# A quantised feed-forward behind two attentions: last norm by token tiles, first inputs prepared in the attention, maxima by quarters, and work shared among DVE, ACT and POOL

## The chip, the cores and the metric

One core of one Trainium2 chip. The metric is the device time of one execution in microseconds (us): 3412.78 before, the median of three runs (3411.16 to 3414.15). PE is the matmul engine; DVE, ACT and POOL work on vectors; SP issues the DMAs. SBUF is the on-chip memory, PSUM holds what PE writes.

## What is computed

Eight batches of 512 tokens, 256 wide, go through four steps; LN is a layer norm without weights:

```
x = x + attention0(LN(x), ctx)      # 16 heads of 64, 1024 context tokens
x = x + experts(LN(x))              # two of eight expert MLPs, chosen by the first token
x = x + attention1(LN(x), ctx)      # 16 heads of 16
x = x + quantised_ffn(LN(x))        # 256 -> 1024 -> 256

def quantised_ffn(x):
    hidden = gelu(a16(x) @ w8(W_in) + b_in)
    return a16(hidden) @ w8(W_out) + b_out
def a16(x):                         # one scale for the whole tensor, all batches
    scale = 32767 / max(|x|)
    return round(x * scale) / scale
```

The maximum in a16 runs over all eight batches. So the feed-forward can't begin with its first matmul before the last batch has left the second attention, nor with its second matmul before hidden is known for every batch.

## The kernel before

**Attention and experts.** Two streams of steps, written as generators, are woven into one order of PE work by a list of run lengths written out by hand (ORDER, weave): the first stream has the first attention of all batches, the second has weights, and for each batch experts, second attention and last norm (rest, L1234). The last batch's second attention is split between the two. PE follows this order; a scheduler orders what is on DVE, ACT, POOL and SP by the steps' place in the program and by what they need.

**project** (L1120) ends the second attention for a tile of 128 tokens (g is 0 to 3): two matmuls (L1123, cacc), and DVE adds the result to x (L1127).

**last_norm** (L1213) runs once a batch's four tiles are done. DVE takes mean and variance (L384, L385). POOL takes the inverse root by three Newton steps on 128x4 values (L387 to L398, about 14 instructions). DVE takes the largest and the smallest x of each token (ends, L1221), POOL subtracts the mean and multiplies by the root (L1223, L1226), which gives the token's largest normed values without norming it. SP stores x to memory (xd, L1231). Later, x is loaded again from there.

**Feed-forward, phase 1.** SP loads the quantised weights wi_q (512 KB, L1287) and wo_q (1 MB, L1289). one_scale (L1269) turns a column of maxima into one scale: a reduction, a transpose on PE, a reduction, a matmul that spreads the value, and the five small DVE instructions of scales (L299 to L302). inputs(b) (L1320) loads xd, norms it (L1325), scales and rounds it (L1333, by adding and keeping a large constant ROUND), splits the integer into two bf16 parts (L1335 and L1338), transposes both on PE (L1346, txq) and copies them to SBUF on ACT (L1347, xTf). For each b there are 32 matmuls 512 wide (L1359, fh), ACT's gelu in eight pieces (L1368) into hid[b], which stays in SBUF, and one DVE reduction of 128x4096 for the maximum (L1378).

**Phase 2**, for each b: load xd again; POOL adds the bias b_out in four instructions (L1388); DVE scales and adds ROUND in two halves (L1392, h); ACT takes ROUND away in four pieces of 128x1024 (L1395, unround); ACT makes hi, rounded to PE's fp32r format (L1401), eight of 128x512; DVE makes the rest, lo (L1402), eight of 128x512; PE does 64 matmuls 256 wide (L1407, fo); DVE joins the product with x (L1416), SP stores the output. The first matmuls need h, unround, hi and lo in this order. The pieces hi and lo lie in a pool of seven buffers (tag "p", L1315). x has three buffers (L125).

Of the kernel before, what the change touches and what calls it, by code (L numbers as in the profile page):

```python
# [8 lines left out]
F32 = mybir.dt.float32  # L9
# [69 lines left out]
def kernel(  # L79
# [75 lines left out]
    xs, xd = {}, {}  # L155
    stats = const.tile([P, B, NT, 2], F32, name="stats")

    ends = const.tile([P, B, 2, NT], F32, name="ends")

    def load_x(b, src=None):  # L160
        t = xpool.tile([P, NT, D], F32, tag="x", name=f"x{b}")
# [68 lines left out]
    cbv_b = wts.tile([P, D], F32, name="cbv_b")  # L230
    cbo_b = wts.tile([P, D], F32, name="cbo_b")
    bo_b = wts.tile([P, D], F32, name="bo_b")

    COPIED = [(0.3, "s", "act", 0.4, "full")]

    def second_weights():

        room = kvp.tile([P, 4, DH, D], F32, tag="cv", name="room", bufs=1)
        nq, nv, no = (room[:, i] for i in range(3))
        nv = nv[:, :, :DC]  # L240
        nc.sync.dma_start(out=nq, in_=c_wq.rearrange("(c p) n -> p c n", p=P))
        nc.sync.dma_start(out=nv, in_=c_wv.rearrange("(c p) n -> p c n", p=P))
        nc.sync.dma_start(out=no, in_=c_wo.rearrange("(c p) n -> p c n", p=P))
        rows = kvp.tile([1, 4, D], F32, tag="ck", name="bias_rows")
        for i, src in enumerate((c_bq, c_bv, c_bo, a_bo)):
            nc.sync.dma_start(out=rows[:, i, :], in_=src.unsqueeze(0))
        yield 30, [(0.5, "s", "dve", 0.3, "one")]
# [12 lines left out]
        for i, dst in ((3, bo_b), (1, cbv_b), (2, cbo_b)):  # L260
            yield 0, [(0.5, "s", "dve", 0.4, "one")]
            t = bank(f"tbo{i}")
            nc.tensor.matmul(t[:, :D], ones_r, rows[:, i, :], start=True, stop=True)
            nc.vector.tensor_copy(dst, t[:, :D])
        done.add("biases")
# [114 lines left out]
    def norm_stats(b, mv, rs):  # L380

        st = small.tile([P, NT, 6], F32, tag="st", name="st")
        for t in range(NT):
            nc.vector.bn_stats(st[:, t, :], xs[b][:, t, :])  # L384
            nc.vector.bn_aggr(mv[:, t, :], st[:, t, :])  # L385
        ve = small.tile([P, NT], F32, tag="ve", name="ve")
        nc.gpsimd.tensor_scalar(ve, mv[:, :, 1], EPS, None, ALU.add)  # L387

        r = small.tile([P, NT], F32, tag="r0", name="r0")
        nc.gpsimd.tensor_scalar(  # L390
            r.bitcast(I32), ve.bitcast(I32), -0.5, float(0x5F3759DF), ALU.mult, ALU.add
        )
        t1 = small.tile([P, NT], F32, tag="t1", name="t1")
        for i in range(3):
            nc.gpsimd.tensor_tensor(t1, r, r, ALU.mult)
            nc.gpsimd.tensor_tensor(t1, t1, ve, ALU.mult)
            nc.gpsimd.tensor_scalar(t1, t1, -0.5, 1.5, ALU.mult, ALU.add)
            nc.gpsimd.tensor_tensor(rs if i == 2 else r, r, t1, ALU.mult)  # L398

    def norm_of(b):  # L400
        mv = small.tile([P, NT, 2], F32, tag="mv", name="mv")
# [535 lines left out]
    def second_attention(b, pairs, last=False):  # L937
# [182 lines left out]
        def project(g, aT):  # L1120
# [4 lines left out]
                )  # L1125
            dst = xs[b][:, g, :]
            nc.vector.tensor_tensor(dst, acc[:, :D], dst, ALU.add)  # L1127

        def scores(p, kt):
            es[p, kt] = exponentials(  # L1130
# [82 lines left out]
    def last_norm(b):  # L1213


        yield 1, [(0, None, "dve", 5.5, None), (0, None, "pool", 4.5, "then")]
        mv = small.tile([P, NT, 2], F32, tag="mv", name="mv")
        norm_stats(b, mv, stats[:, b, :, 1])
        nc.vector.tensor_copy(stats[:, b, :, 0], mv[:, :, 0])
        for i, op_ in enumerate((ALU.max, ALU.min)):  # L1220
            nc.vector.tensor_reduce(ends[:, b, i, :], xs[b], AX.X, op_)  # L1221
        for i in range(2):
            nc.gpsimd.tensor_tensor(  # L1223
                ends[:, b, i, :], ends[:, b, i, :], stats[:, b, :, 0], ALU.subtract
            )
            nc.gpsimd.tensor_tensor(  # L1226
                ends[:, b, i, :], ends[:, b, i, :], stats[:, b, :, 1], ALU.mult
            )
# [63 lines left out]
    bor = fw.tile([1, D], F32, name="bor")  # L1292
    nc.sync.dma_start(out=bor, in_=f_bo.unsqueeze(0))

    amax_x = fw.tile([P, 1], F32, name="amax_x")
    nc.vector.tensor_reduce(
# [9 lines left out]
    t = bank("bbo")  # L1306
    nc.tensor.matmul(t[:, :D], ones_r, bor, start=True, stop=True)
    bo_b = fw.tile([P, D], F32, name="bo_b")
    nc.vector.tensor_copy(bo_b, t[:, :D])

    hp = ffn.enter_context(tc.tile_pool(name="hid", bufs=1))
    amax_h = fw.tile([P, B], F32, name="amax_h")

    def parts_of(shape, dtype, name):
        return hp.tile(shape, dtype, tag="p", name=name, bufs=7)  # L1315
# [1 line left out]

    COARSE = 512 * ROUND

    def inputs(b):  # L1320

        load_x(b, xd[b])
        xn = parts_of([P, NT, D], F32, f"xn_{b}")
        for t in range(NT):
# [5 lines left out]
                ALU.subtract,  # L1330
                ALU.mult,
            )
        nc.vector.tensor_scalar(xn, xn, s_x, ROUND, ALU.mult, ALU.add)  # L1333
        xq = parts_of([P, 2, NT, D], BF16, f"xq_{b}")
        nc.vector.tensor_scalar(  # L1335
            xq[:, 0], xn, COARSE - ROUND, COARSE, ALU.add, ALU.subtract
        )
        nc.vector.scalar_tensor_tensor(  # L1338
            xq[:, 1], xn, ROUND, xq[:, 0], ALU.subtract, ALU.subtract
        )  # L1340
# [11 lines left out]
    for b in range(B):  # L1352
        hid = hp.tile([P, NF, S], F32, tag=f"h{b}", name=f"h{b}")
        for f2 in range(NF // 2):
# [11 lines left out]
            for j in range(2):  # L1366
# [5 lines left out]
                    bias=bi[:, f : f + 1],  # L1372
                    scale=sc_i[:, f : f + 1],
                )
            if f2 == 1 and b + 1 < B:
                following = inputs(b + 1)
        xT = following
        nc.vector.tensor_reduce(  # L1378
            amax_h[:, b : b + 1], hid, AX.XY, ALU.max, apply_absolute_value=True
        )  # L1380
        hids.append(hid)

    s_h, inv_h = one_scale(amax_h, 32767.0, "h")
    for b in range(B):
        hid = hids[b]
        load_x(b, xd[b])
        for i in range(NT):
            nc.gpsimd.tensor_tensor(xs[b][:, i, :], xs[b][:, i, :], bo_b, ALU.add)  # L1388
        acc = ps_s.tile([P, 2, 512], F32, tag="s", name=f"fo_{b}")
        for half in range(2):  # L1390
            h = hid[:, half * 4 : half * 4 + 4, :]
            nc.vector.tensor_scalar(h, h, s_h, ROUND, ALU.mult, ALU.add)  # L1392
        for f2 in range(NF // 2):
            h = hid[:, 2 * f2 : 2 * f2 + 2, :]
            nc.scalar.activation(h, h, AF.Identity, bias=unround)  # L1395
            hi = parts_of([P, 2, S], F32R, f"hi_{b}_{f2}")
            lo = parts_of([P, 2, S], F32R, f"lo_{b}_{f2}")
            for j in range(2):
# [6 lines left out]
                for t in range(NT):  # L1405
                    for u in range(2):
# [8 lines left out]
        dst = xs[b].rearrange("p t d -> p (t d)")  # L1415
        nc.vector.scalar_tensor_tensor(  # L1416
            dst, acc.rearrange("p i n -> p (i n)"), inv_h, dst, ALU.mult, ALU.add
        )
        nc.sync.dma_start(out=out[b].rearrange("(t p) d -> p t d", p=P), in_=xs[b])
    ffn.close()  # L1420


# [49 lines left out]
```

## Time and profile before

| | us |
|---|---|
| median of 3 runs | 3412.78 |
| the profiled execution | 3413.37 |
| its span | 3411.5 |
| last sum on x in the attention, start | 3233.99 |
| first fh of phase 1 | 3250.4 |
| last gelu ends | 3317.9 |
| first h of phase 2 | 3324.9 |
| last lo ends | 3403.1 |

Times within the profile count from the span's start, so the phases behind the attention take 177.5 us of it. Groups of instructions are shown as: line, engine, operation, output <- inputs by the program's names, shapes, count, then busy time, the mean duration of one in ns, and after the second bar how long the engine had been idle just before them and what ended that idle time. Timelines give the start, the length of a row of instructions and their number. L12 is line 12 of the kernel. The profiled execution's granted TensorE clock was 0.974 of full speed.

### The profile page before, as it was taken

To read this page: it belongs to the slowest core of one execution; us is meant where nothing else is said; L and a number is where in the kernel's file an instruction comes from. 1 tells how busy PE (TensorE), PEld (TensorE's weight loads), DVE (VectorE), ACT (ScalarE), POOL (GpSimd) and SP (SyncE) were. 2 spreads that over 40 slices of the span, in tenths; PEclk is the share of its full clock that TensorE was granted. 3 is DMA by queue.
4 is the path that set the end of the run, shared out by engine and by line. 5 is a ranking of instruction groups with operands and counts; after the bars stand their busy time and mean duration, and the time that the engine had idled before them with its cause. 6 is when DMAs were issued, how large, how long until landed. Compare 5 with 4: busy or idle time off the path is not lost.

```text
span 3411.5 us, 59285 instructions
## 1 busy us (share of the span) xinstructions
PE 3183.9 (93%) x24293; PEld 1789.0 (52%) x24293; DVE 2045.0 (60%) x2583; ACT 1857.9 (54%) x2589; POOL 1282.3 (38%) x1260
## 2 busy tenths in 40 slices
PE   7899999999999999999999999999999999978887
PEld 4455555555455555555545554555555555544347
DVE  3654566546665476655665466654766456656688
ACT  4554456544556455554655455554555546544578
POOL 4355522454234622355224542345223543311002
PEclk9999999999999999999999999999999999988989
DMA  2010111011110111111110111101111111012112
GB/s 86 26 32 21 45 33 37 27 41 41 38 35 27 43 32 36 35 44 29 32 51 14 41 41 38 41 26 38 32 41 32 41 32 29 14 44 62 50 57 81
DMA packets 102649, 132.00 MB, mean 39 GB/s; under 512 B 19807, under 2 KB 82028, under 8 KB 102252
## 3 DMA queue, kind: packets, MB, share of 16 engines
q1 hardware_dynamic: 102380, 128.22, 13.7%
q8 instruction: 192, 3.15, 0.4%
q14 instruction: 77, 0.63, 0.1%
HBM read 67.34 MB, written 9.96 MB: 23 GB/s over the span
## 4 chain that ended last, share of the span: by engine, by line
PE 74%; DVE 12%; ACT 6%; POOL 3%; issue 2%; DMA 1%; SPq 1%; ACTq 0%; DVEq 0%; POOLq 0%
PE s L728 15%; PE av L699 11%; PE cav L1079 6%; PE t L676 6%; DVE cmx L531 5%; PE acc L486 5%; PE pv L512 4%; PE s_c L562 3%; PE pq L602 3%; PE pk L512 3%; ACT e L741 2%; ACT e_c L567 2%; PE sm_c L524 2%; PE s_c L565 2%; PE pv L514 2%
## 5 line engine op out<-in xcount | busy, mean ns | idle before, releaser
L758 POOL TENSOR_TENSOR e<-e,share 128x1024 f32<-128x1024 f32 x512 | 958.9, 1894 | 1559.1 <-DVE share L755 1528.0
L741 ACT ACTIVATE e<-s,least 128x1024 f32<-128x1024 f32 x512 | 569.6, 1113 | 621.3 <-DVE least L739 590.0
L739 DVE TENSOR_REDUCE least<-s 128x1 f32<-128x1024 f32 x512 | 603.2, 1219 | 229.5 <-PE s L728 226.4
L531 DVE TENSOR_REDUCE cmx<-sm_c 128x2 f32<-128x1024 f32 x512 | 602.1, 1219 | 169.8 <-PE sm_c L524 169.2
L728 PE MATMUL s<-k,q 64*128 64x512 f32 x2048 | 586.6, 624 | 23.0 <-ACT et L690 8.8
L567 ACT ACTIVATE e_c<-s_c 128x1024 f32<-128x1024 f32 x512 | 499.7, 1024 | 112.9 <-PE s_c L565 101.8
L699 PE MATMUL av<-et,v 128*64 128x256 f32 x4096 | 472.2, 384 | 0.7 <-ACT et L690 0.7
L688 DVE COPY et<-t 128x1024 f32<-128x1024 f32 x256 | 312.8, 1222 | 230.4 <-PE t L676 228.5
L699 PEld LDWEIGHTS av<-et,v 128*64 128x64 f32 x4096 | 284.4, 137 | 219.4 <-issue 67.9
L728 PEld LDWEIGHTS s<-k,q 64*128 64x128 f32 x2048 | 237.1, 191 | 221.1 <-issue 118.1
L676 PEld LDWEIGHTS t<-ident,e 64*128 64x128 f32 x8192 | 294.4, 141 | 93.9 <-issue 68.2
L690 ACT COPY et<-t 128x1024 f32<-128x1024 f32 x256 | 260.1, 1016 | 151.4 <-PE t L676 149.9
L676 PE MATMUL t<-ident,e 64*128 64x64 f32 x8192 | 313.7, 227 | 18.1 <-ACT e_c L567 12.1
L562 PE MATMUL s_c<-cq,ck 64*128 64x512 f32 x1024 | 248.5, 476 | 16.1 <-ACT e_c L567 10.7
L524 PE MATMUL sm_c<-ck,cq 64*128 64x512 f32 x1024 | 228.5, 442 | 25.9 <-DMA ck<-ckl 12.5
L1079 PE MATMUL cav<-e_c,cv 128*32 128x512 f32 x2048 | 248.2, 599 | 2.2 <-DVE cmx L531 1.9
L755 DVE RECIPROCAL share<-total 128x2 f32<-128x2 f32 x256 | 42.5, 166 | 298.2 <-ACT e L741 297.8
L565 PE MATMUL s_c<-m_rows,m_ones 64*128 64x512 f32 x1024 | 208.6, 396 | 2.7 <-DMA m_rows<-mr_c 2.6
L562 PEld LDWEIGHTS s_c<-cq,ck 64*128 64x128 f32 x1024 | 99.3, 187 | 165.2 <-issue 39.4
L524 PEld LDWEIGHTS sm_c<-ck,cq 64*128 64x128 f32 x1024 | 98.8, 189 | 107.5 <-DVE cmx L531 38.4
L512 PE MATMUL pv<-wv,c 128*128 128x256 f32 x512 | 131.2, 399 | 3.7 <-DMA wv<-in_L_xattn_w_kv_dram 2.4
L512 PE MATMUL pk<-c,wk 128*128 128x512 f32 x256 | 126.8, 618 | 4.5 <-DVE et L688 2.7
(202 smaller groups left out, 3382.9 us busy)
## 6 DMA issues: line engine op xcount, KB each, us to landing
cq<-cqs SPq DMA_DIRECT2D x256, 64.0 KB
ck<-ckh SPq DMA_DIRECT2D x112, 128.0 KB
ck<-ckl SPq DMA_DIRECT2D x112, 128.0 KB
wq<-in_L_xattn_w_q_dram SPq DMA_DIRECT2D x32, 256.0 KB
wo<-in_L_xattn_w_out_dram SPq DMA_DIRECT2D x32, 256.0 KB
w<-in_L_ffn_W_dram SPq DMA_DIRECT2D x32, 256.0 KB
x<-xd SPq DMA_DIRECT2D x16, 512.0 KB
ctx<-in_ctx_dram SPq DMA_DIRECT2D x16, 384.0 KB
```

The costliest lines, as they stand in the source:

```text
L512: nc.tensor.matmul(out, lhs, rhs, start=first, stop=False, skip_group_check=True)
L524: nc.tensor.matmul(s[:, h, :], q[half, tok(i)], k[half, g * 512 : (g + 1) * 512], start=True, stop=True,)
L531: nc.vector.tensor_reduce(mx[:, :, i, g], s, AX.X, ALU.max)
L562: nc.tensor.matmul(s[:, h, :], k[half, tok(kt)], q[half, :], start=True, stop=False)
L567: nc.scalar.activation(e, s, AF.Exp, scale=scale)
L676: nc.tensor.transpose(t[:, w, h, kt, :], es[n, i][h][half, tok(4 * u + kt)], ident[half, half],)
L699: nc.tensor.matmul(av[h * AD : (h + 1) * AD, : S // 2], v[m][:, 4 * u + kt, (at + h) * AD : (at + h + 1) * AD], turned[n, j, u][:, h, kt]. ...
L728: nc.tensor.matmul(s[h][:, g, :], q[n][half, tok(i)], k[n][half, g * 512 : (g + 1) * 512], start=True, stop=True,)
L739: nc.vector.tensor_reduce(least[:, h : h + 1], s[h], AX.XY, ALU.min)
L741: nc.scalar.activation(e, s[h].rearrange("p g n -> p (g n)"), AF.Exp, bias=least[:, h : h + 1], scale=-1.0, accum_out=total[:, h : h + 1],)
L758: nc.gpsimd.tensor_tensor(e, e, share[:, h : h + 1].to_broadcast([P, L]), ALU.mult)
L1079: nc.tensor.matmul(av[col : col + SL, :], va[:, v : v + SL], es[p, kt][:, h, :], start=(i == 0), stop=(i == NK // 4 - 1),)
```

## The change

Four edits.

1. **Last norm of batch 7 by token tiles.** project takes statistics and ends of each tile right behind its sum. The root and the ends' correction are on DVE for this batch (12 to 16 small instructions); for the other batches they stay on POOL.
2. **First inputs in the attention.** x of batch 0 is loaded again while batch 7 is in the second attention, normed on DVE, and transposed as float on PE behind the last attention step; ACT copies it. inputs(0) then only scales and splits, in two halves, and needs no transpose.
3. **Maxima by quarters.** The reduction of 128x4096 becomes four of 128x1024, each behind its two gelus.
4. **Phase 2 shared.** The bias is added on POOL at the end of last_norm and the sum stored a second time (xe); phase 2 loads xe, and POOL's adds and the bias matmul at the boundary go. For batches 1 to 7 the unround of pieces 1 and 3 is on POOL. For batches 0 to 6 the join becomes an ACT multiplication into a buffer of the seven (part) and a POOL sum. The last batch keeps DVE's join, in two halves with two stores. Batch 0's h comes in quarters.

In the order of the engines' instructions the attention is otherwise as before. On SP, wi_q and wo_q now stand behind the two stores of batch 7's x, before they stood ahead of or between them. On POOL, the order of phase 2 is: unrounds of batches 1 and 2 and the first of 3, the sum of batch 0, the other of 3, those of 4 and 5 and the first of 6, the sum of batch 1, the rest of the unrounds, the other sums.

```diff
@@ root, split off norm_stats
+    def root(mv, rs, engine):
...
+        if engine is nc.vector:
+            engine.tensor_scalar(ve, ve, -0.5, None, ALU.mult)
         for i in range(3):
+            engine.tensor_tensor(t1, r, r, ALU.mult)
+            engine.tensor_tensor(t1, t1, ve, ALU.mult)
+            if engine is nc.vector:
+                engine.scalar_tensor_tensor(to, t1, 1.5, r, ALU.add, ALU.mult)
+            else:
+                engine.tensor_scalar(t1, t1, -0.5, 1.5, ALU.mult, ALU.add)
+                engine.tensor_tensor(to, r, t1, ALU.mult)
@@ project
             nc.vector.tensor_tensor(dst, acc[:, :D], dst, ALU.add)
+            if b == B - 1:
+                nc.vector.bn_stats(last_st[:, g, :], dst)
+                nc.vector.bn_aggr(last_mv[:, g, :], last_st[:, g, :])
+                for i, op_ in enumerate((ALU.max, ALU.min)):
+                    nc.vector.tensor_reduce(ends[:, b, i, g : g + 1], dst, AX.X, op_)
@@ last_norm
+        if b == B - 1:
+            mv = last_mv
+            root(mv, stats[:, b, :, 1], nc.vector)
+            engine = nc.vector
+        else:
+            mv = small.tile([P, NT, 2], F32, tag="mv", name="mv")
+            norm_stats(b, mv, stats[:, b, :, 1])
+            engine = nc.gpsimd
...
         nc.sync.dma_start(out=xd[b], in_=xs[b])
+        xe[b] = dram.tile([P, NT, D], F32, name=f"xe{b}")
+        for i in range(NT):
+            nc.gpsimd.tensor_tensor(xs[b][:, i, :], xs[b][:, i, :], fbo_b, ALU.add)
+        nc.sync.dma_start(out=xe[b], in_=xs[b])
@@ second_stream, before and behind the last second_attention
+        load_x(0, xd[0])
+        for t in range(NT):
+            nc.vector.tensor_scalar(xs[0][:, t, :], xs[0][:, t, :],
+                stats[:, 0, t, 0:1], stats[:, 0, t, 1:2], ALU.subtract, ALU.mult)
         yield from second_attention(B - 1, range(NP // 2, NP))
+        for c in range(DH):
+            for i in range(NT):
+                nc.tensor.transpose(t[:, c, tok(i)], xs[0][:, i, tok(c)], ident)
+        nc.scalar.copy(first_xT, t)
@@ inputs
+        if b == 0:
+            xT = parts_of([P, DH, 2, S], BF16, f"xTf_{b}")
+            for c in range(DH):
+                parts_of_integers(xT[:, c, 0, :], xT[:, c, 1, :], firsts[0][:, c, :])
+            return xT
@@ phase 1
+            nc.vector.tensor_reduce(amax_h[:, b, f2 : f2 + 1],
+                hid[:, 2 * f2 : 2 * f2 + 2, :], AX.XY, ALU.max, apply_absolute_value=True)
-        nc.vector.tensor_reduce(
-            amax_h[:, b : b + 1], hid, AX.XY, ALU.max, apply_absolute_value=True
-        )
@@ phase 2
-        load_x(b, xd[b])
-        for i in range(NT):
-            nc.gpsimd.tensor_tensor(xs[b][:, i, :], xs[b][:, i, :], bo_b, ALU.add)
+        load_x(b, xe[b])
+        n = 2 if b == 0 else 4
+        for f in range(0, NF, n):
+            h = hid[:, f : f + n, :]
             nc.vector.tensor_scalar(h, h, s_h, ROUND, ALU.mult, ALU.add)
...
-            nc.scalar.activation(h, h, AF.Identity, bias=unround)
+            if f2 % 2 and b > 0:
+                nc.gpsimd.tensor_scalar(h, h, -ROUND, 1.0, ALU.add, ALU.mult)
+            else:
+                nc.scalar.activation(h, h, AF.Identity, bias=unround)
...
+        if b + 1 < B:
+            part = parts_of([P, 2, 512], F32, f"part_{b}")
+            nc.scalar.mul(part, acc, inv_h)
+            dst = xs[b].rearrange("p (i t) d -> p i (t d)", i=2)
+            nc.gpsimd.tensor_tensor(dst, part, dst, ALU.add)
+            nc.sync.dma_start(out=out[b].rearrange("(t p) d -> p t d", p=P), in_=xs[b])
+            continue
```

More of the change, by code (lines that the diff above doesn't have):

```diff
@@ L153 @@
     nc.vector.tensor_tensor(fold, ident[:, 0:AD], ident[:, AD:P], ALU.add)
-    xs, xd = {}, {}
+    xs, xd, xe, firsts = {}, {}, {}, []
     stats = const.tile([P, B, NT, 2], F32, name="stats")
     ends = const.tile([P, B, 2, NT], F32, name="ends")
+    last_st = const.tile([P, NT, 6], F32, name="last_st")
+    last_mv = const.tile([P, NT, 2], F32, name="last_mv")
     def load_x(b, src=None):
@@ L232 @@
     bo_b = wts.tile([P, D], F32, name="bo_b")
+    fbo_b = wts.tile([P, D], F32, name="fbo_b")
     COPIED = [(0.3, "s", "act", 0.4, "full")]
@@ L246, in second_weights @@
             nc.sync.dma_start(out=rows[:, i, :], in_=src.unsqueeze(0))
+        row_f = kvp.tile([1, D], F32, tag="cq", name="bias_row_f")
+        nc.sync.dma_start(out=row_f, in_=f_bo.unsqueeze(0))
         yield 30, [(0.5, "s", "dve", 0.3, "one")]
@@ L264, in second_weights @@
             nc.vector.tensor_copy(dst, t[:, :D])
+            if i == 2:
+                t = bank("tbo4")
+                nc.tensor.matmul(t[:, :D], ones_r, row_f, start=True, stop=True)
+                nc.vector.tensor_copy(fbo_b, t[:, :D])
         done.add("biases")
@@ L385, in norm_stats @@
             nc.vector.bn_aggr(mv[:, t, :], st[:, t, :])
+        root(mv, rs, nc.gpsimd)
+    def root(mv, rs, engine):
         ve = small.tile([P, NT], F32, tag="ve", name="ve")
-        nc.gpsimd.tensor_scalar(ve, mv[:, :, 1], EPS, None, ALU.add)
+        engine.tensor_scalar(ve, mv[:, :, 1], EPS, None, ALU.add)
         r = small.tile([P, NT], F32, tag="r0", name="r0")
-        nc.gpsimd.tensor_scalar(
+        engine.tensor_scalar(
             r.bitcast(I32), ve.bitcast(I32), -0.5, float(0x5F3759DF), ALU.mult, ALU.add
@@ L393, in norm_stats @@
         t1 = small.tile([P, NT], F32, tag="t1", name="t1")
+        if engine is nc.vector:
+            engine.tensor_scalar(ve, ve, -0.5, None, ALU.mult)
         for i in range(3):
[L395 to L398, printed above, removed]
+            to = rs if i == 2 else r
+            engine.tensor_tensor(t1, r, r, ALU.mult)
[5 more added lines that the diff above has]
+                engine.tensor_tensor(to, r, t1, ALU.mult)
     def norm_of(b):
@@ L1216, in last_norm @@
         yield 1, [(0, None, "dve", 5.5, None), (0, None, "pool", 4.5, "then")]
-        mv = small.tile([P, NT, 2], F32, tag="mv", name="mv")
-        norm_stats(b, mv, stats[:, b, :, 1])
+        if b == B - 1:
[6 more added lines that the diff above has]
+            engine = nc.gpsimd
+            for i, op_ in enumerate((ALU.max, ALU.min)):
+                nc.vector.tensor_reduce(ends[:, b, i, :], xs[b], AX.X, op_)
         nc.vector.tensor_copy(stats[:, b, :, 0], mv[:, :, 0])
-        for i, op_ in enumerate((ALU.max, ALU.min)):
-            nc.vector.tensor_reduce(ends[:, b, i, :], xs[b], AX.X, op_)
         for i in range(2):
-            nc.gpsimd.tensor_tensor(
+            engine.tensor_tensor(
                 ends[:, b, i, :], ends[:, b, i, :], stats[:, b, :, 0], ALU.subtract
             )
-            nc.gpsimd.tensor_tensor(
+            engine.tensor_tensor(
                 ends[:, b, i, :], ends[:, b, i, :], stats[:, b, :, 1], ALU.mult
@@ L1253, in second_stream @@
         yield lambda: (B - 1, "values") in done
-        yield from second_attention(B - 1, range(NP // 2, NP))
+        load_x(0, xd[0])
+        for t in range(NT):
+            nc.vector.tensor_scalar(
+                xs[0][:, t, :],
+                xs[0][:, t, :],
+                stats[:, 0, t, 0:1],
+                stats[:, 0, t, 1:2],
+                ALU.subtract,
+                ALU.mult,
+            )
+        yield from second_attention(B - 1, range(NP // 2, NP))
+        first_xT = work.tile([P, DH, S], F32, tag="xT2", name="first_xT", bufs=1)
+        firsts.append(first_xT)
+        t = ps_s.tile([P, DH, S], F32, tag="s", name="txf")
+        for c in range(DH):
+            for i in range(NT):
+                nc.tensor.transpose(t[:, c, tok(i)], xs[0][:, i, tok(c)], ident)
+        nc.scalar.copy(first_xT, t)
     with tc.manual_schedule(engines={mybir.EngineType.PE}):
@@ L1291 @@
     nc.vector.tensor_copy(identb, ident)
-    bor = fw.tile([1, D], F32, name="bor")
-    nc.sync.dma_start(out=bor, in_=f_bo.unsqueeze(0))
     amax_x = fw.tile([P, 1], F32, name="amax_x")
@@ L1305 @@
     nc.vector.tensor_scalar(sc_i, inv_w[0], inv_x, None, ALU.mult)
[L1306 to L1309, printed above, removed]
     hp = ffn.enter_context(tc.tile_pool(name="hid", bufs=1))
-    amax_h = fw.tile([P, B], F32, name="amax_h")
+    amax_h = fw.tile([P, B, NF // 2], F32, name="amax_h")
     def parts_of(shape, dtype, name):
@@ L1318, with parts_of_integers @@
     COARSE = 512 * ROUND
+    def parts_of_integers(hi, lo, xn):
+        nc.vector.tensor_scalar(xn, xn, s_x, ROUND, ALU.mult, ALU.add)
+        nc.vector.tensor_scalar(hi, xn, COARSE - ROUND, COARSE, ALU.add, ALU.subtract)
+        nc.vector.scalar_tensor_tensor(lo, xn, ROUND, hi, ALU.subtract, ALU.subtract)
     def inputs(b):
+        if b == 0:
[3 more added lines that the diff above has]
+            return xT
         load_x(b, xd[b])
@@ L1332, in inputs @@
             )
-        nc.vector.tensor_scalar(xn, xn, s_x, ROUND, ALU.mult, ALU.add)
         xq = parts_of([P, 2, NT, D], BF16, f"xq_{b}")
-        nc.vector.tensor_scalar(
-            xq[:, 0], xn, COARSE - ROUND, COARSE, ALU.add, ALU.subtract
-        )
-        nc.vector.scalar_tensor_tensor(
-            xq[:, 1], xn, ROUND, xq[:, 0], ALU.subtract, ALU.subtract
-        )
+        parts_of_integers(xq[:, 0], xq[:, 1], xn)
         xT = parts_of([P, DH, 2, S], BF16, f"xTf_{b}")
@@ L1374 @@
                 )
+            nc.vector.tensor_reduce(
+                amax_h[:, b, f2 : f2 + 1],
+                hid[:, 2 * f2 : 2 * f2 + 2, :],
+                AX.XY,
+                ALU.max,
+                apply_absolute_value=True,
+            )
             if f2 == 1 and b + 1 < B:
@@ L1377 @@
         xT = following
-        nc.vector.tensor_reduce(
-            amax_h[:, b : b + 1], hid, AX.XY, ALU.max, apply_absolute_value=True
-        )
         hids.append(hid)
-    s_h, inv_h = one_scale(amax_h, 32767.0, "h")
+    s_h, inv_h = one_scale(amax_h.rearrange("p b f -> p (b f)"), 32767.0, "h")
     for b in range(B):
         hid = hids[b]
-        load_x(b, xd[b])
-        for i in range(NT):
-            nc.gpsimd.tensor_tensor(xs[b][:, i, :], xs[b][:, i, :], bo_b, ALU.add)
+        load_x(b, xe[b])
         acc = ps_s.tile([P, 2, 512], F32, tag="s", name=f"fo_{b}")
-        for half in range(2):
-            h = hid[:, half * 4 : half * 4 + 4, :]
+        n = 2 if b == 0 else 4
+        for f in range(0, NF, n):
+            h = hid[:, f : f + n, :]
             nc.vector.tensor_scalar(h, h, s_h, ROUND, ALU.mult, ALU.add)
@@ L1414 @@
                         )
[L1415 to L1419, printed above, removed]
+        if b + 1 < B:
[5 more added lines that the diff above has]
+            continue
+        for i in range(2):
+            dst = xs[b][:, 2 * i : 2 * i + 2, :]
+            nc.vector.scalar_tensor_tensor(
+                dst.rearrange("p t d -> p (t d)"),
+                acc[:, i, :],
+                inv_h,
+                dst.rearrange("p t d -> p (t d)"),
+                ALU.mult,
+                ALU.add,
+            )
+            nc.sync.dma_start(
+                out=out[b, i * 256 : (i + 1) * 256].rearrange("(t p) d -> p t d", p=P), in_=dst
+            )
     ffn.close()
```

## The prediction

> **What bounds the kernel now.** I read the page first: PE is busy 93% of the span and 74% of the chain that ended last, but that is the attention, whose order the change hardly touches. So I cut the end of the span into five stretches with the windows view: the boundary between attention and feed-forward, its first phase, the maximum between the phases, the second phase to the end of ACT's steady work, and the rest.
>
> ```profile
> core 0: us, PE busy (x) PEld busy (x) DVE busy (x) ACT busy (x) POOL busy (x), PEclk, DMA share, GB/s
> 3234.00:3250.40 16.40, 4.09 (x21) 2.65 (x22) 12.29 (x31) 1.90 (x2) 3.56 (x18) 0.50 0.63 213
> 3250.40:3317.90 67.50, 64.90 (x368) 31.81 (x367) 54.81 (x50) 58.88 (x72) 8.35 (x12) 0.96 0.15 50
> 3317.90:3324.90 7.00, 0.92 (x3) 0.58 (x3) 5.53 (x8) 0.00 (x0) 0.00 (x0) 0.71 0.01 2
> 3324.90:3380.00 55.10, 44.51 (x322) 42.25 (x323) 54.17 (x62) 53.41 (x70) 18.34 (x14) 0.88 0.23 77
> 3380.00:3411.50 31.50, 23.48 (x192) 22.66 (x190) 20.72 (x27) 19.71 (x26) 4.63 (x7) 0.97 0.24 84
> ```
>
> Phase 1 is PE's (64.9 of 67.5 us). In phase 2's first 55.1 us DVE (54.2) and ACT (53.4) are both full; PE is not. The 16.4 us and the 7.0 us are chains in which PE has 4.1 and 0.9 us of work. So phase 2 is 86.6 us long (3324.9 to 3411.5), and what decides it is what DVE, ACT and POOL can do side by side. The groups by form (busy us, mean ns) give the prices, first those of the window from 3229 on, then POOL's of the whole run:
>
> ```profile
> L1402 DVE SCALAR_TENSOR_TENSOR lo<-h,inv_w,hi 128x512 fp32r<-128x512 f32 x64 | 46.6, 787 | 0.0
> L1401 ACT ACTIVATE hi<-h,inv_w 128x512 fp32r<-128x512 f32 x64 | 41.9, 714 | 1.1 <-ACT hi L1401 0.7 <-ACT h L1395 0.2
> L1395 ACT ACTIVATE h<-h,unround 128x1024 f32<-128x1024 f32 x32 | 35.8, 1142 | 8.4 <-DVE h L1392 8.4
> L1388 POOL TENSOR_TENSOR x<-x,bo_b 128x256 f32<-128x256 f32 x32 | 31.3, 1011 | 118.3 <-DMA x<-xd 118.3
> L1392 DVE TENSOR_SCALAR h<-h,sh 128x2048 f32<-128x2048 f32 x16 | 20.6, 1308 | 0.0
> ```
>
> ```profile
> L758 POOL TENSOR_TENSOR e<-e,share 128x1024 f32<-128x1024 f32 x512 | 958.9, 1894 | 1559.1 <-DVE share L755 1528.0 <-DMA ck<-ckl 16.1 <-PE t L676 6.5
> L409 POOL TENSOR_SCALAR xn<-x,mv,rs 128x256 f32<-128x256 f32 x96 | 116.1, 1222 | 1.9
> ...
> L397 POOL TENSOR_SCALAR t<-t 128x4 f32<-128x4 f32 x96 | 18.6, 194 | 7.7
> L910 POOL TENSOR_SCALAR b<-b 128x256 f32<-128x256 f32 x8 | 6.9, 863 | 0.1
> L909 POOL TENSOR_TENSOR b<-b,b 128x256 f32<-128x256 f32 x8 | 5.8, 722 | 86.2 <-DMA b<-in_L_ffn_b_dram 86.2
> ```
>
> Two things stand in them. A tensor_scalar of 128x256 on POOL takes 1.222 us with two operations and 0.863 with one, against 0.722 for a sum of two tensors. And L1388's adds take 1.011 on the mean, where the same shape takes 0.722 elsewhere: something holds them up in phase 2. The timelines show what, first POOL's at two places (start, us, instructions), then DVE's at the same two:
>
> ```profile
> 110.17 3.96 POOL L758 TENSOR_TENSOR e<-e,share 128x1024 f32<-128x1024 f32 x2 [4.40 <-DVE share L755]
> ...
> 3347.50 6.34 POOL L1388 TENSOR_TENSOR x<-x,bo_b 128x256 f32<-128x256 f32 x4 [38.96 <-DMA x<-xd]
> ```
>
> ```profile
> 110.40 3.88 DVE L306 TENSOR_SCALAR wT<-wT,s_w 128x256 f32<-128x256 f32 x2
> ...
> 3350.81 0.75 DVE L1402 SCALAR_TENSOR_TENSOR lo<-h,inv_w,hi 128x512 fp32r<-128x512 f32 x1
> 3351.49 1.77 DVE L1392 TENSOR_SCALAR h<-h,sh 128x2048 f32<-128x2048 f32 x1
> 3353.17 1.88 DVE L1402 SCALAR_TENSOR_TENSOR lo<-h,inv_w,hi 128x512 fp32r<-128x512 f32 x2
> ```
>
> Two L306 on DVE, 0.6 us when POOL is still, take 3.88 us, exactly as long as POOL's two e. Four adds take 6.34 us instead of 2.8 while DVE runs h and lo, and h takes 1.77 instead of 1.27. Singly: one add ends at 3352.16, h (begun at 3351.49) ends 1.09 us after it, the next add ends 0.59 after h, the next lo 0.54 after that. **They run one after the other, not side by side.** That holds for DVE's work from SBUF in h and lo; DVE's reads of PSUM and its reductions keep their time beside POOL (L739 is 1.221 us beside an e and 1.218 alone). Small tensor_scalars of POOL are held too: an L397 at 3237.3, beside DVE's L1325, took 0.32 instead of 0.194.
>
> **Phase 2, part by part.** DVE's exclusive work: h, 14 halves at 1.2 and 4 quarters at 0.68 (L365's 128x1024 row), 19.5; lo, 64 at a pitch of 0.665, 42.6; together 62. The last 8 joins of 1.28 from PSUM are gone but for the last batch. POOL's: 32 adds of bias are gone; 7 sums of 128x1024 come in, at L758's 1.894 = 13.3; and 14 of the 32 unrounds come over from ACT, each a two-operation tensor_scalar of 128x1024, T.
>
> No row shows T. From below: L910's one operation scaled as the sums scale (0.863 x 1.894/0.722) = 2.26. From above: L409 with L397's 0.194 as the fixed part, 0.194 + 1020 x 1.028/252 = 4.36. With the fixed part that the sums show (0.722 and 1.894 give 0.33), L409 gives 0.33 + 0.89 x 4 = 3.9. T has two operations, as L409, so I take 3.9: 14 x 3.9 = 54.6.
>
> Side by side the engines would have: DVE 63, POOL 68, ACT 65 (10.1 for batch 0, 6 x 8.0, 7.0; ACT loses 14 x 1.04 and gains 7 copies of about 1.0), PE 60 (512 matmuls at the full clock's pitch of 0.118). In a row, DVE and POOL have 62 + 13.3 + 54.6 = 130. There is work for both nearly all the time, since DVE's order runs the h's far ahead. After the last lo come 8.4 us as before (3403.1 to 3411.5), for PE's last matmuls, the join and the store. 130 + 8.4 = 138 against 86.6: **+52**. With T at its bounds: 84 + 14 x 2.26 = 116, +29; 84 + 14 x 4.36 = 145, +58.
>
> At this place a rule of the Trainium skill differs from the row. L910 has one input and needs 0.863 us, more than the two-input sum's 0.722. "GPSIMD Engine Reference", section "Engine selection", says that one-input elementwise work there is roughly at line rate and only two-input work about twice slower than VectorE; this trace has it the other way round. If the rule held, T as an estimate would be lo's rate, 1.33, and phase 2 84 + 18.6 = 103, +16.
>
> **The boundary.** Before, first fh starts at 3250.4, 16.1 us after the last sum on x (3233.99 + 0.42). The chain: bn, POOL's root 3236.2 to 3240.8, the scale to 3243.9, three passes to 3246.5, transposes, ACT copy of 1.9. After: the statistics of three token tiles are there earlier; root and ends are some 16 small DVE instructions at the pitch of L299 to L302 (0.19) = 3.1 in place of 4.6; and after the scale (3.0 as before) only 0.77 until the first half's hi is ready. 3234.9 + 3.1 + 3.0 + 0.8 = 3241.8. But wi_q, which SP issued at 3233.96, now stands behind xe7: xd7's store lands about 3237.2 (2.8 after its issue, as at 706.20, where the next load was released at 708.97), four POOL adds of 0.725 end at 3240.1, then xe7 and wi_q are issued; at 3 to 4 us for its 512 KB (an estimate from that store's 2.8) it lands at 3244. So that is late next, and fh starts at 3244.3: **-6** (bounds -8, if wi_q lands sooner; -3, if both stores and wo_q's 1 MB slow it). The eight transposes and the ACT copy of x0 lie in PE's idle 7.7 us before the maximum (3233.9 to 3241.6); without that cover, +2.
>
> **Phase 1 and the maximum.** The last reduction of 4.42 us becomes one of 1.22 (L739's row): -3.2. PE waited 3.1 us for DVE's xq, some of it behind a 4.4 us reduction: -1.3. The 32 quarters cost DVE 1.6 more in all, under PE. **-4.5** (bounds -3 and -6).
>
> **The attention.** Each of seven last norms gets 2.9 us of POOL adds and a store that waits for them on SP. At the one at 706 POOL is done at +6.2, has two e at +7.0 to +10.8 and the next root at +14.0: 2.9 fit with 1.2 to spare. Behind xe on SP stand the x load (+2.8, now about +12) and the loads of wk and wo (+6.1, +9.7), whose first readers come at +53 and later. Without the cover it would be 7 x 2.9 = 20. Four norms of x0 (0.41 each) and eight small reductions fall where DVE is now and then last, one matmul and copy at the start: **+1** (0 to +3).
>
> **Sum:** 52 - 6 - 4.5 + 1 = +42.5 on the profiled execution's 3413.4: 3456. The median of the runs, 3412.8, is 0.6 lower.
>
> **The rivals.**
> 1. POOL's tensor_scalar is no dearer than its sum (T 1.33, lo's pitch twice, to 1.894, L758). For it: with immediates in place of L409's pointers it may be a better form. Against: L910 has an immediate. Phase 2 103 to 110.5; 3420 to 3428.
> 2. Faster: POOL's tensor_scalar, of one tensor, does not exclude DVE, only its sums do. For it: no row has a large tensor_scalar of POOL beside an h or lo. Against: L397's 0.32. Then phase 2 is 62 + 13.3 + 8.4 = 84, POOL's 68 lie beside it: -2.6 - 6 - 4.5 + 1 = -12, 3401. It decides where the exclusive part of T is below 0.86 us: 84 + 14 x 0.86 = 96, the 86.6 of before and the 9.5 that the other terms give back.
> 3. Worse: ACT's in-order queue stands at the hi of a batch behind POOL's late unround or sum, DVE has no lo, and the row has gaps; 2 us for each of seven batches, +14: 3470 and over.
>
> **How the numbers follow.** Forecast 0.72 (3430 to 3470, from T's bounds and the other terms'), rival 1 0.10, rival 2 0.11, rival 3 0.07. Range 3418 to 3471: it leaves out rival 2 and most of rival 3. Under 0.2% (6.8 us) a measurement here can't tell from no change: faster 0.12, same 0.05, slower 0.83.
>
> **What would show it.** The group of POOL's unround: T, alone and in place. DVE's h and lo: means over 1 us if they wait for POOL, 0.75 and 1.3 if not. ACT idle in phase 2 with POOL named as what ended it. First fh at 3244 with wi_q's DMA as its releaser. A last reduction of 1.2. The last cacc within 3 us of 3233.9. The prediction is wrong if T is under 2, or if lo keeps 0.75 us beside T.

## The result and the profile after

The changed kernel takes 3454.51 us (median of 4 runs, 3453.2 to 3455.24) against 3413.47 before: ratio 1.012, interval 1.0107 to 1.0133. It is 1.2% slower, and 1.5 us from the forecast. **The total was right, and most of its terms were not**: the span grew by 40.9 us, 38.4 of them in phase 2, where 52 were forecast and by another mechanism, and 9.6 in the attention, where 1 was. That the sum came so near is luck: phase 2 was put 13.6 us too long, the attention 8.6, phase 1 2.9 and the boundary 0.6 too short.

| us, from the two traces | before | after | measured | forecast |
|---|---|---|---|---|
| attention, to the last sum on x | 3233.99 | 3243.55 | +9.6 | +1 |
| boundary, to the first fh | 16.4 | 11.0 | -5.4 | -6 |
| phase 1, to the end of the last gelu | 67.5 | 69.1 | +1.6 | -1.3 |
| maximum, to the first h | 7.1 | 3.8 | -3.3 | -3.2 |
| phase 2, to the end | 86.6 | 125.0 | +38.4 | +52 |

The windows view of the changed kernel, cut at the boundary, at the end of phase 1, at the first h and twice in phase 2:

```profile
core 0: us, PE busy (x) PEld busy (x) DVE busy (x) ACT busy (x) POOL busy (x), PEclk, DMA share, GB/s
3244.00:3254.60 10.60, 1.28 (x7) 0.70 (x6) 7.57 (x35) 1.01 (x1) 2.76 (x4) 0.66 0.67 234
3254.60:3323.50 68.90, 64.62 (x368) 31.00 (x368) 63.35 (x83) 58.36 (x72) 0.00 (x0) 0.98 0.21 71
3323.50:3327.45 3.95, 0.82 (x3) 0.58 (x3) 2.40 (x9) 0.15 (x1) 0.00 (x0) 0.82 0.02 4
3327.45:3381.00 53.55, 33.23 (x192) 30.00 (x192) 50.53 (x43) 36.88 (x45) 28.81 (x16) 0.73 0.12 40
3381.00:3440.00 59.00, 40.48 (x266) 38.66 (x267) 32.60 (x36) 29.28 (x45) 11.78 (x5) 0.87 0.21 71
```

Before, DVE and ACT were full in most of phase 2. Now, in the 59 us from 3381 on, nobody is: DVE 32.6, ACT 29.3, PE 40.5, POOL 11.8. A forecast by sums of busy time can't see such a stretch; it is made of waits. The groups of phase 2 say whose:

```profile
L1457 DVE SCALAR_TENSOR_TENSOR lo<-h,inv_w,hi 128x512 fp32r<-128x512 f32 x64 | 64.0, 1057 | 29.4 <-ACT hi L1456 29.0 <-issue 0.2
...
L1448 POOL TENSOR_SCALAR h<-h 128x1024 f32<-128x1024 f32 x14 | 22.3, 1602 | 96.2 <-ACT hi L1456 81.9 <-DVE h L1444 14.3
...
L1474 POOL TENSOR_TENSOR x<-part,x 128x1024 f32<-128x1024 f32 x7 | 18.4, 2630 | 51.1 <-ACT part L1472 51.1
...
L1472 ACT ACTIVATE part<-fo,invh 128x1024 f32<-128x1024 f32 x7 | 7.8, 1110 | 37.7 <-PE fo L1462 37.7
```

POOL's unround takes 1.6 us with its waits (1.24 at the least), not 3.9. lo has grown from 0.787 to 1.057: DVE does wait for POOL. And there is a ring: ACT's part waits 37.7 us for PE, DVE's lo 29.0 us for ACT's hi. ACT's timeline over one batch, from 3392 to 3412, and PE's at the same place (start, length, instructions) show how it turns:

```profile
3393.57 1.11 ACT L1472 ACTIVATE part<-fo,invh 128x1024 f32<-128x1024 f32 x1 [7.24 <-PE fo L1462]
3394.58 5.00 ACT L1456 ACTIVATE hi<-h,inv_w 128x512 fp32r<-128x512 f32 x8
3407.02 1.11 ACT L1472 ACTIVATE part<-fo,invh 128x1024 f32<-128x1024 f32 x1 [7.44 <-PE fo L1462]
```

```profile
3395.34 0.38 PE L1462 MATMUL fo<-wo_q,hi 128*128 128x256 f32 x1 [1.81 <-ACT hi L1456]
3397.77 0.58 PE L1462 MATMUL fo<-wo_q,lo 128*128 128x256 f32 x1 [2.05 <-DVE lo L1457]
```

ACT works in order. Its part of batch b needs the last matmul of batch b, and behind it stand all eight hi of batch b+1. So the next batch can't begin before this one has ended: 13.4 us a batch, in which ACT stands still for 7.4. Of the 2.05 us before the first lo's matmul, 1.65 are the lock, as the prediction's "one after the other" between DVE and POOL is called from here on: POOL's sum begins at 3394.82, and DVE's first lo takes 2.39 us in place of 0.74.

PE, which the ring waits for, is slow at first, too. Two stretches of the windows view, with its columns, show it:

```profile
3397.70:3401.10 3.40, 3.33 (x15) 3.33 (x16) 3.33 (x6) 1.88 (x4) 0.00 (x0) 0.50 0.46 154
3401.10:3407.00 5.90, 5.88 (x50) 5.67 (x48) 1.42 (x2) 0.00 (x0) 0.00 (x0) 1.00 0.26 89
```

At a granted clock of 0.50 its matmuls follow each other every 0.213 us, at 1.00 every 0.119. For some 15 matmuls that makes 1.4 of a batch's 13.4 us.

### The profile page after: what moved, and what is told of

It is laid out like the page before. It is cut to its first block, busy times and chain, and to the rows that moved or that the text cites. A ratio compares the mean times of both kernels' runs of the same rounds, so it can differ in the third digit from the quotient of the medians.

```text
span 3452.4 us, 59313 instructions
## 1 busy us (share of the span) xinstructions
PE 3198.2 (93%) x24285; PEld 1797.9 (52%) x24285; DVE 2061.9 (60%) x2628; ACT 1850.1 (54%) x2582; POOL 1309.5 (38%) x1263
## 5 line engine op out<-in xcount | busy, mean ns | idle before, releaser
L717 PEld LDWEIGHTS av<-et,v 128*64 128x64 f32 x4096 | 284.9, 138 | 221.2 <-issue 70.6
```

Of the source, the lines that this page charges most:

```text
L717: nc.tensor.matmul(av[h * AD : (h + 1) * AD, : S // 2], v[m][:, 4 * u + kt, (at + h) * AD : (at + h + 1) * AD], turned[n, j, u][:, h, kt]. ...
```

## The experiments

An experiment starts from the changed kernel unless its expectation names another. Lengths of phase 2 are from the first h to the end of the span.

**Whose is phase 2: the queue or the lock?** Four kernels: the join back on DVE, the unround back on ACT, both back, and part written later.

```diff
# join_dve
-            part = parts_of([P, 2, 512], F32, f"part_{b}")
-            nc.scalar.mul(part, acc, inv_h)
-            nc.gpsimd.tensor_tensor(dst, part, dst, ALU.add)
+            nc.vector.scalar_tensor_tensor(dst, acc, inv_h, dst, ALU.mult, ALU.add)
# unround_act
-            if f2 % 2 and b > 0:
+            if False:
                 nc.gpsimd.tensor_scalar(h, h, -ROUND, 1.0, ALU.add, ALU.mult)
# both_back: these two. late_part: part and sum of a batch become join(b)
         for f2 in range(NF // 2):
+            if f2 == 2 and b > 0:
+                join(b - 1)
```

> The changed kernel with one thing undone: the join of batches 0 to 6 is DVE's again (one instruction from PSUM), the unround stays shared with POOL. Phase 2 of the changed kernel took 125.0 us (3327.45 to 3452.4) and POOL was busy for only 41 of them, so the sum of the prediction (DVE and POOL in a row, an unround of 3.9 us on POOL) does not explain it: one unround there took 1.24 us at the least. Theory Q (ACT's queue): part, ACT's half of the join, waits for a batch's last matmul and stands ahead of the next batch's hi, so that no batch overlaps the next; without it phase 2 falls to DVE's 72 us and 14 x 1.24 us of locks and the 8.4 us behind the last lo, 95 to 100 us, and the time to about 3427. Theory L (only the lock between DVE and POOL): 7 sums of 1.9 us go and 7 joins of 1.28 come, phase 2 about 121, the time about 3450.

> The changed kernel with all unrounds on ACT again; the join stays divided between ACT and POOL. Theory Q: the wait stays, each batch still takes about 13.4 us, phase 2 118 to 125, the time 3448 to 3455. Theory L: 14 unrounds of 1.24 us leave the row, phase 2 about 107, the time about 3437.

> The changed kernel with part and POOL's sum of a batch written behind the hi of the first two pieces of the next batch instead of ahead of them: same instructions, other order on ACT. Theory Q: ACT no longer stands at part, the batches overlap, phase 2 falls to the row of DVE and POOL, 62 + 17 + 13 + 8 = 101 to 105 us, the time to about 3432. Theory L: no change, 3454. A third theory, S (part takes a ninth place of seven buffers): no change either, since the buffers are the same.

> The changed kernel with join and unround both as before; the bias stays in the stored x, so POOL does nothing in phase 2. All theories: DVE's 72 us, ACT's 73, no locks, phase 2 80 to 86 us, the time 3409 to 3416. What is left against the kernel before is then the sum of the other edits: +9.6 us up to the last sum of the attention, -5.4 from there to the first fh, -1.6 from there to the first h, by the two traces.

| | time | ratio to before | phase 2 | DVE busy in it | ACT | POOL |
|---|---|---|---|---|---|---|
| before | | | 86.6 | 74.9 | 73.1 | 23.0 |
| changed | 3454.51 | 1.012 | 125.0 | 87.4 | 66.3 | 40.6 |
| unround on ACT | 3442.83 | 1.0086 (1.0069 to 1.0103) | 114.8 | 76.2 | 80.4 | 22.0 |
| part late | 3423.11 | 1.003 (1.0017 to 1.0042) | 96.3 | 88.2 | 66.4 | 39.3 |
| join on DVE | 3413.39 | 1.000 (0.9991 to 1.001) | 85.0 | 79.2 | 60.1 | 26.3 |
| both back | 3408.93 | 0.999 (0.998 to 1.0) | 80.8 | 72.1 | 72.8 | 0 |

With part two pieces later, and with it only the sum and the store that follow it, 28.6 us of phase 2 go. That is the queue, with some of the clock in it, which was granted at 0.89 in this phase 2 and at 0.81 in the changed kernel's. DVE's busy time stays (88.2 after 87.4); what goes is its standing still, from 37.6 to 8.1. What is left in that kernel is the lock: DVE, whose own work there is about 64 us (62 of h and lo, the last join), is busy for 88 of 96 us, some 24 of them, by that difference, waiting for POOL with an instruction begun. The expected 101 to 105 us were too many. Theory S (the buffers) said no change and falls as the main cause.

Neither theory gave join_dve's number: 85.0 against 95 to 100 and 121. Q's estimate still added every unround to DVE's row. DVE's 79.2 there against 72.1 with both back makes the 14 unrounds' cost 7.1 us, half a microsecond each. unround_act's 114.8 lies between the two expectations and tells little alone; with both back beside it, it says that the join's share costs 34 us without any unround on POOL.

**Is it only the place of the join?** Unrounds on ACT, the join shared, part late.

> All unrounds on ACT, and the join shared by ACT and POOL with part written behind the first two pieces' hi of the next batch. Phase 2 so far: both shares 125.0, join's alone 114.8, unround's alone 85.0, none 80.8, both with a late part 96.3. Theory Q + L: with the queue's wait gone the join's share costs the lock of 7 sums against 7 joins less on DVE, and 7 part more on ACT: 86 to 90, the time about 3417. If the division of the join costs its 34 us whatever its place, 105 or more.

Measured 3423.4 (1.0031, 1.0018 to 1.0043), phase 2 95.45. The place made 19.3 of the 34 us (114.8 to 95.5), and the expected 86 to 90 were missed. Two groups show why:

```profile
L1467 ACT ACTIVATE hi<-h,inv_w 128x512 fp32r<-128x512 f32 x64 | 42.0, 712 | 5.8 <-POOL x L1443 5.7
...
L1443 POOL TENSOR_TENSOR x<-part,x 128x1024 f32<-128x1024 f32 x7 | 28.3, 4036 | 137.0 <-ACT part L1441 137.0
```

POOL's sum takes 4.0 us on the mean where it takes 1.9 alone, and 9.64 the first time (3340.21), while DVE's queue is full: DVE's h and lo follow each other without a pause to 3347.65, and the sum ends 2.2 us behind that. The lock goes back to DVE, and POOL gets in only when DVE leaves it. part keeps one of the seven buffers so long, and ACT's hi waits 5.7 us for it. So theory S was not all wrong: the buffers do cost, once the sum is starved. In the later batches a batch takes 10.06 us, which is ACT's own work with a part in it (4 x 1.04 + 8 x 0.61 + 1.0 = 10.0). Shared this way the join brings nothing even without the queue: it takes 9 us from DVE and puts 7 on ACT, which was as full. What the buffer alone costs wasn't tried.

**The price of an unround on POOL, and the lock, by themselves.** Behind the last store, instructions whose results go nowhere:

```diff
+    g.tensor_scalar(y, y, -ROUND, 1.0, ADD, MULT)       # y 128x1024, each form twice
+    g.tensor_scalar(y, y, -ROUND, None, ADD)
+    g.tensor_scalar(y, y, stats[..0:1], stats[..1:2], SUBTRACT, MULT)
+    ... the same on w = y[:, 0:256], but (w, w, 0.5, None, MULT) as the second; then y + y
+    4 x g.tensor_scalar(z, y, -ROUND, 1.0, ADD, MULT)   # beside 8 of DVE, of lo's form
```

> The kernel with wi_q first and, behind its last store, 18 more POOL and 8 more DVE instructions whose results go nowhere; only their durations are read. POOL alone first, each form twice: 128x1024 with two immediates (add, mult), with one (add), with two pointers (subtract, mult); 128x256 with two immediates, with one, with two pointers; a sum of 128x1024. Then four of the first form beside eight DVE instructions of lo's form. From the runs so far: two immediates on 1024 about 1.03, pointers on 256 1.22 and one immediate on 256 0.86 as in the attention. If the form decides, one immediate on 1024 is 2 us or more and two pointers over 4; if a fixed cost decides, all three are near 1 us more than the same on 256 times one. Beside DVE: with the lock 8 lo and 4 unrounds take 8 x 0.66 + 4 x 1.03 = 9.4 us together, without it 5.3.

POOL's groups behind the last store (L1500, L1506 two immediates; L1502, L1508 one; L1504, L1510 two pointers):

```profile
L1504 POOL TENSOR_SCALAR x<-x,stats 128x1024 f32<-128x1024 f32 x2 | 7.6, 3784 | 0.2
L1515 POOL TENSOR_SCALAR h<-x 128x1024 f32<-128x1024 f32 x4 | 5.7, 1417 | 0.3
L1502 POOL TENSOR_SCALAR x<-x 128x1024 f32<-128x1024 f32 x2 | 5.6, 2777 | 0.2
L1512 POOL TENSOR_TENSOR x<-x 128x1024 f32<-128x1024 f32 x2 | 3.8, 1892 | 0.2
L1510 POOL TENSOR_SCALAR x<-x,stats 128x256 f32<-128x256 f32 x2 | 2.4, 1223 | 0.2
L1500 POOL TENSOR_SCALAR x<-x 128x1024 f32<-128x1024 f32 x2 | 2.1, 1044 | 158.2 <-DMA out_dram<-x 158.2
L1508 POOL TENSOR_SCALAR x<-x 128x256 f32<-128x256 f32 x2 | 1.7, 856 | 0.2
L1506 POOL TENSOR_SCALAR x<-x 128x256 f32<-128x256 f32 x2 | 0.8, 403 | 0.2
```

The form decides. 1024 elements with two immediates take 1.044 us, with one immediate 2.777, with two pointers 3.784. The last is the 3.9 of the forecast, to 3%: it was the price of another instruction. The four unrounds and eight lo together took 8.5 us (3424.31 to 3432.82; 9.4 with the lock, 5.3 without): DVE's lo took 0.74 alone and 1.52 beside an unround. An unround and a lo come every 1.44 us, where 1.04 and 0.66 in a row would be 1.70. So they exclude each other for most of their length, and rival 2 of the prediction falls.

**The attention's 9.6 us.** Between batch 5's last sum and batch 6's first, the changed kernel lost 6.7 us against the kernel before (from 1.7 late to 8.5). DVE's, SP's and PE's timelines there:

```profile
2700.48 0.74 DVE L1291 TENSOR_SCALAR x<-x,stats 128x256 f32<-128x256 f32 x2 [8.52 <-DMA x<-xd]
2701.13 1.22 DVE L514 TENSOR_TENSOR x<-acc,x 128x1024 f32<-128x1024 f32 x1
```

```profile
2693.95 0.33 SPq L1265 DMA_DIRECT2D xe<-x  x1
2696.63 0.33 SPq L165 DMA_DIRECT2D x<-xd  x1
```

```profile
2702.41 3.78 PE L746 MATMUL s<-k,q 64*128 64x512 f32 x6 [5.66 <-DVE x L514]
```

The norm of x0 (L1291) was moved into the attention and stands in DVE's queue already here, five hundred microseconds before it is needed and not, as the change has it, while batch 7 is in the second attention. It waits for x0's load, which is issued at 2696.63, behind the second store of batch 5, which waits for POOL's bias adds. Behind the norm stands L514, a sum of the first attention that PE waits for.

```diff
# no_xe: one store; the bias is added in phase 2 again; fbo_b lies as in fbo_const below
# tied_back (with both_back's phase 2): the norm stands behind the second attention's
# steps in the program and can't be placed early
+        nc.vector.tensor_scalar(z0, last_mv[:, 1, 0:1], 0.0, None, MULT)
+        nc.vector.tensor_scalar(s0, stats[:, 0], z0, None, ADD)   # and the norm reads s0
```

> The changed kernel without the second store: x without bias is stored once, POOL adds the bias in phase 2 as before; phase 2 is not what is looked at. In the changed kernel DVE stood 8.5 us at the norm of x0 behind batch 5's last norm, waiting for x0's load, and a sum that the first attention needs stood behind it; batch 5's last sum was 1.7 us later than before, batch 6's first 8.5. Theory N (two edits together): the norm of x0 sits early in DVE's queue, and its load waits on SP behind the second store; without the second store the load is there in time and the 6.7 us are gone: the step between those two sums is under 1.5 us. Rival: the norm's own place costs it, whatever the stores: the step stays 6 to 7 us.

> Both shares of phase 2 undone, and x0's norm tied by a small DVE instruction to the statistics of the last batch's third tile, so that it can't stand in DVE's queue before that. Second store kept. Theory N: the step behind batch 5's last norm falls to under 1 us, the time by 4 to 6 us against the kernel with both shares undone (3408.9): 3403 to 3405. Rival (POOL's sums and the second store delay the attention by themselves): the step stays 4 us or more, 3408.

The step is -0.6 us without the second store and -0.1 with the norm tied, against +6.7 and, with both shares back, +6.4. Either edit alone is harmless; together they cost 6.5 us. tied_back takes 3404.67 (0.997, 0.9958 to 0.9982). no_xe took 3449.71 in its single run, with phase 2 at 129.6. Where the attention begins its way differs from execution to execution by up to 5 us (batch 0's first sum came 0.5 us earlier to 4.6 later than before, in kernels alike up to there), so 1.6 of the 9.6 say nothing. A second step, of 1.4 us, lies between batch 6's second and third sum, where PE waits for the load of keys (ck): 11.5 us after 9.9, 10.1 in no_xe, 10.6 with the norm tied. Its cause stays open.

**The boundary.** The first fh did wait for wi_q, 2.7 us, in the changed kernel:

```profile
3254.59 5.21 PE L1408 MATMUL fh<-xTf,wi_q 128*128 128x512 bf16 x16 [2.72 <-DMA wi_q<-wi_d]
```

wi_first issues the last second store behind wi_q and wo_q; fbo_const besides moves the broadcast bias into the pool that lives throughout.

```diff
# wi_first
+    nc.sync.dma_start(out=xe[B - 1], in_=xs[B - 1])   # behind wo_q's load
# fbo_const
-    fbo_b = wts.tile([P, D], F32, name="fbo_b")
+    fbo_b = const.tile([P, D], F32, name="fbo_b")
```

> As the tied kernel, with the second store of the last batch issued behind wi_q and wo_q. In the changed kernel PE waited 2.7 us for wi_q before the first fh, and wi_q was issued at 3250.2, behind that store. If wi_q is what is late, the boundary falls from 11 to 12 us to about 8.5 to 9.5 (what DVE's chain leaves), the time by 2 to 3 us. If DVE's chain is as late as wi_q, under 1 us.

> As the kernel with wi_q first, but the broadcast bias fbo_b lies in the pool that lives through the whole kernel, not in the attention's. In that kernel both DVE's cast of identb and SP's issue of wi_q came at 3240.7, the end of POOL's four bias adds (3237.92 to 3240.68), though neither reads them. Theory M: identb and wi_q get memory that the attention's pool frees, and the last reader of that pool is POOL's bias add; with fbo_b elsewhere the wait goes, the boundary falls from 10.55 to about 7.9 (what the kernel without second store had), the time by 2 to 3 us, to about 3401. Rival: the cast waits for the lock between DVE and POOL: no change.

wi_first gave 3403.31 (0.9974, 0.9962 to 0.9986) and a boundary of 10.55 after 12.1; no more, though the store was out of the way. DVE and SP in that kernel:

```profile
3240.72 0.23 DVE L1349 CAST identb<-ident 128x128 bf16<-128x128 f32 x1 [2.66 <-POOL x L1264]
```

```profile
3240.71 0.32 SPq L1344 DMA_DIRECT2D wi_q<-wi_d  x1
```

Both come at the end of POOL's four bias adds (3237.92 to 3240.68), and neither reads what they write. wi_q and identb lie in memory that the attention's pool gives back, and the adds are its last readers, by fbo_b. With fbo_b elsewhere wi_q is issued at 3237.92, before the last sum on x (3237.99), and the boundary is 8.75. The 7.9 expected were missed where POOL's adds now lie: they start at 3243.39, and beside them two DVE steps behind the scale take 0.88 and 0.69 us (0.47 and 0.22 in wi_first). The time is 3401.14 (0.9962, 0.9948 to 0.9975), the fastest of all kernels here: the change without both shares of phase 2, its norm tied, its bias moved. Its interval and wi_first's overlap, so this step is shown by the trace and not by the time. Phase 1 takes back 0.7 us of each of the two steps (69.1, 69.9, 70.6), as its first gelu comes later behind the first fh (5.3, 6.0, 6.7).

**Quarters only for the last batch.**

> As the kernel with wi_q first, but maxima by quarters for the last batch alone; batches 0 to 6 have one reduction of 128x4096 again. Phase 1 took 69.1 us with quarters and 67.5 without. If the quarters delay PE (more DVE time, xq later), phase 1 falls by 1 to 2 us and so does the time. If the 1.6 us come from the slow start (first fh waiting, ACT's table load), no change.

3403.8 (0.997, 0.996 to 0.9981) against wi_first's 3403.31: no change. Phase 1 is 1.0 us shorter and the maximum 0.9 longer. The slow start shows in ACT's timelines, first of the kernel before, then of the changed one:

```profile
3250.37 1.28 ACT L1368 ACT_TABLE_LOAD   x1
3254.01 1.45 ACT L1368 ACTIVATE h<-fh,bi,sc_i 128x512 f32<-128x512 f32 x2 [2.36 <-PE fh L1359]
```

```profile
3258.51 1.28 ACT L1417 ACT_TABLE_LOAD   x1 [13.14 <-DVE xq L1367]
3259.80 2.78 ACT L1417 ACTIVATE h<-fh,bi,sc_i 128x512 f32<-128x512 f32 x4
```

ACT loads the table of gelu once, ahead of the first gelu. Before, the load ran beside the first fh and was done 2.4 us before the first gelu had its input. In the changed kernel it starts 3.9 us behind the first fh, and the gelu follows at its end. Why it starts so late stays open.

## Why the prediction was right, and where it was not

- **Phase 2, +52 forecast, +38.4 measured.** Two steps failed. "T has two operations, as L409, so I take 3.9": L409 has pointers, the unround immediates, and T is 1.04. Both bounds, 2.26 and 4.36, were too high as well, since L910's form with one immediate is the slow one too: 2.78 on 1024. The step that L409's and L910's price per element carries over to any form is what was wrong; rival 1 doubted it for just that reason; the rows with two immediates, L390 and L397, have four elements. That work on one input is dearer on POOL than on two, as the prediction read from L910, is so for that form and for pointers; with two immediates it is 1.04 against the sum's 1.89. By the prediction's own sign, "wrong if T is under 2", this part of it was wrong. With T at 1.04 the prediction's own sum, 84 + 14 x 1.04 = 99, would have been 26 us short of the 125 measured, about the queue's 28.6. The other failed step is "there is work for both nearly all the time". DVE stood still for 37.6 us, since ACT's queue had part ahead of the next batch's hi. Rival 3 had ACT's in-order queue as its mechanism, but named POOL's late work and not the join, and gave it 2 us a batch where the queue alone cost 4. T cost the forecast about 40 us too much (14 x 2.86) and the queue 28.6 too little, so these two errors cancelled for the most part, by luck.
- **Exclusion of DVE and POOL: right**, shown by forms (8.5 us for what would be 5.3) and by lo's growth. As a sum in a row it is an upper bound: in join_dve an unround cost DVE half a microsecond, not its whole length.
- **Attention, +1 forecast, +9.6 measured.** "Behind xe on SP stand the x load" was seen, and that its reader comes much later was wrong: the reader had been moved forward by the same change, into DVE's queue. "Four norms of x0 (0.41 each)" priced their work and not their wait.
- **Boundary, -6 forecast, -5.4 measured**, with wi_q's DMA as releaser as said. That it is late because it stands behind xe7's store was half the cause: the store out of the way brought 1.5 us, and the wait on POOL's adds through the pool's memory, which held it and the cast of identb, another 1.8.
- **Last reduction 1.2: right**, 7.1 to 3.8. That PE would get 1.3 us back in phase 1 was wrong: phase 1 grew by 1.6. Its first gelu already comes 1.6 us later behind the first fh (5.2 after 3.6), with ACT's table load of 1.28 us right ahead of it, and its last one still does. last_quarters gives 1.0 us of it back and loses 0.9 at the maximum.
- **The bias out of phase 2 was not priced.** With both shares back phase 2 is 80.8 against 86.6. POOL's 23 us of adds are gone from it, and DVE is busy for 72.1 instead of 74.9. Batch 0's quarters and the halved last join are in it too, and 2.0 of the 5.8 us lie behind the last lo (8.4 before, 6.4 now). What each is worth wasn't tried.

## What to carry to other kernels

An instruction that waits for the end of one batch must not stand in an in-order queue ahead of the work that starts the next; here two pieces later was worth 28.6 us, with what the higher clock of that run gave. Price an instruction by a row of its very form (immediates or pointers, one operation or two), or measure it, before its duration is multiplied by 14. When work is moved early, ask of each moved instruction what it waits for at its new place and who stands behind it; and when memory is handed on from one stage to the next, the last reader of the old stage holds up the first writers of the new one.

## What the runs showed of the hardware

- POOL's tensor_scalar on 128x1024 floats takes 1.044 us with two immediates, 2.777 with one, 3.784 with two pointers; on 128x256 0.403, 0.856 and 1.22 (forms). On 128x1024 a second operation that does nothing (times 1.0) makes it 2.7 times faster.
- Between DVE and POOL the lock is not shared evenly when DVE's queue is full: a sum of 1.89 us took 9.64 (late_join_only, 3340.21), an unround of 1.04 us took 4.61 in join_dve, begun at 3344.70: it ended 1.0 us after DVE had turned to a join from PSUM at 3348.32.
